# Adaptive-layernorm block: down products taken two or four token tiles at a time, their 64-row remainders on different rows, the last layernorm in two parts, stores from four buffers

## The chip, the cores and the metric

The kernel runs on one NeuronCore of one Trainium2 chip. The metric is the device time of one execution in microseconds. Lower is better.

## The reference

One transformer block with adaptive layernorm, for a batch of 2 sequences of 1024 tokens of 256 features, in float32 throughout. A vector `c` gives shift, scale and gate rows by one product; then come causal attention with 16 heads of 128 and a gated feed-forward part whose weights are integers with a scale for each output row. Cut to what matters:

```python
sa, ca, ga, sb, cb, gb = silu(c) @ wmod            # ga, gb kept at least 0.25 from zero
h = layernorm(x) * (1 + ca) + sa
x = x + ga * attention(h, Wq, bq, Wk, bk, Wv, bv, Wo, bo)   # rotary, causal softmax
h = layernorm(x) * (1 + cb) + sb
gate = silu(h @ ((wq_gate - 128) * s_gate[:, None]).T)      # 256 -> 704
up = h @ ((wq_up - 128) * s_up[:, None]).T                  # 256 -> 704
x = x + gb * ((gate * up) @ ((wq_down - 128) * s_down[:, None]).T)   # 704 -> 256
```

The hidden width is 704 = 5 x 128 + 64. That remainder of 64 is what much of the change is about.

## The kernel before, in words

The order of all work is written out by hand: every engine executes its instructions in the order in which the program text issues them, and a wait holds up all that stands behind it on the same engine. SP's queue issues the loads, the transposing copies of the attention and the stores; ACT's queue issues some loads.

*Attention.* The main loop (L644 to L684) goes over 32 units (batch, pair of heads, head) and in each over eight query tiles of 128 tokens. For each tile, TensorE makes scores, DVE masks them and finds the maximum, ACT takes the exponential, DVE turns 32x32 blocks, and SP's copies finish the transposition into `pT`. `values` multiplies it with v into the bank `po`, `project_out` adds the output product to the residual `x[b]` (L482, on DVE). Projections for the next unit, and pieces listed in `extras`, fill the loop.

*Feed-forward.* Tokens go in four blocks of 512: (batch 0, block 0), (0, 1), (1, 0), (1, 1). For each block `ln_turn` (L206) transposes the normalized tiles `xn` on TensorE into two banks of `ps_a`, and DVE applies the modulation (L217) into `h2`. `hidden(b, blk, c)` (L495) makes chunk c of the 704 hidden features for 512 tokens: gate and up products (L508), silu on ACT (L522), product of both on DVE (L523) into `gT`. The last chunk, c = 5, holds 64 gate rows and 64 up rows in one bank, and its product (L520) goes to rows 0 to 63 of `gT`. `down(b, blk, j)` (L525) multiplies the `gT` of one token tile of 128 with the scaled down weights `wdT` in six contractions, five over 128 rows and one over 64, into a bank `pd`; DVE adds the residual into `yo` (L538), and SP stores it (L539). `yo` comes from the two buffers "r1" of the pool `rot`.

The down weights reach the chip with their last 64 rows repeated (L775), and `ffn_down_scale` scales all 128 rows of every chunk, so rows 64 to 127 of `wdT`'s last chunk hold a copy of rows 0 to 63 already.

*Banks.* `bank` (L466) hands out four accumulation banks in turn: one of `ps_y`, one of `ps_o`, two of `ps_a`. The transposes of `ln_turn` take the same two of `ps_a`. The gate and up products of the tail have two double banks of `ps_sc`.

*The tail* (L686 to L718) starts when the last unit's scores are done, near 985 us. It interleaves `hidden(0, 1, c)` with the last output products, then does `values` of the last unit (TensorE from 1001.25 us on), chunk 4, four output products, chunk 5. Then DVE takes the statistics of all eight token tiles of batch 1 (`ln_stats`), ACT the root for all (`ln_sqrt`), and the four down tiles of block (0, 0) run with `ln_scale` and `ln_turn` of (1, 0) between. In the chunks of block (1, 0) stand `ln_turn` of (1, 1), after chunk 0, and one down tile of (0, 1) after each of the chunks 1 to 4; in the chunks of (1, 1) one down tile of (1, 0) each in the same places. The four down tiles of (1, 1) end the program:

```python
        for c in range(NF):
            hidden(1, 1, c)
            if c in (1, 2, 3, 4):
                down(1, 0, c - 1)
        for j in range(4):
            down(1, 1, j)
```

Block (0, 0) of the feed-forward part runs its `hidden` chunks inside the last attention unit (L677).

Of the kernel before, what the change touches and what calls it, by code (L numbers as in the profile page):

```python
# [11 lines left out]
F32 = mybir.dt.float32  # L12
I32 = mybir.dt.int32
AF = mybir.ActivationFunctionType
ALU = mybir.AluOpType
PSUM = bass.MemoryType.PSUM

P = 128
B, S, D = 2, 1024, 256
H, DH = 16, 128  # L20
HID = 704
NT = S // P
# [15 lines left out]
def adaln_block(ctx: ExitStack, tc: tile.TileContext, a, cos_d, sin_d, out):  # L38
# [427 lines left out]
    def bank(name):  # L466

        pool, tag = banks[turn[0] % 4]
        turn[0] += 1
        return pool.tile([P, 512], F32, tag=tag, name=name)  # L470

    def project_out(u, t, late=False):

        b, g, h = u
        if t % 4 == 0:
            nc.vector.reciprocal(rdens[u][:, t : t + 4], dens[u][:, t : t + 4])  # L476
        name = f"py_{b}{g}{h}{t}"
        py = bank(name) if late else ps_y.tile([P, 512], F32, tag="y", name=name)
        nc.tensor.matmul(  # L479
            py[:, :D], outs[u][:, ts(t, P)], weights[b, g]["o"][:, h, :], start=True, stop=True  # L480
        )
        nc.vector.scalar_tensor_tensor(  # L482
            x[b][:, t, :], py[:, :D], rdens[u][:, t : t + 1], x[b][:, t, :], ALU.mult, ALU.add
        )
# [10 lines left out]
    def hidden(b, blk, c, late=True):  # L495
        if c == 0:
            gTs[b, blk] = fpool.tile([P, NF, QB], F32, tag="f", name=f"gT_{b}{blk}")
        last = c == NF - 1
        if late:
            pg = ps_sc.tile([P, S], F32, tag="sc", name=f"pgu_{b}{blk}{c}")  # L500
            pgs = [pg[:, ts(j, QB)] for j in range(2)]
        else:
            pgs = [
                ps_a.tile([P, 512], F32, tag="a", name=f"pgu_{b}{blk}{c}{j}") for j in range(2 - last)
            ]
        for pg, n in zip(pgs, ("gate",) if last else ("gate", "up")):
            for k in range(KC):
                nc.tensor.matmul(  # L508
                    pg,
                    wT["last"][:, k, :] if last else wT[n][:, k, ts(c, P)],  # L510
                    h2s[b, blk][:, k, :],
                    start=(k == 0),
                    stop=(k == KC - 1),
                )
        sg = ppool.tile([P, QB], F32, tag="p", name=f"sg_{b}{blk}{c}")
        if last:

            m = HID - FULL
            nc.scalar.activation(sg[m:], pgs[0][:m], AF.Silu)
            nc.vector.tensor_tensor(gTs[b, blk][:m, c, :], sg[m:], pgs[0][m:], ALU.mult)  # L520
        else:
            nc.scalar.activation(sg, pgs[0], AF.Silu)  # L522
            nc.vector.tensor_tensor(gTs[b, blk][:, c, :], sg, pgs[1], ALU.mult)  # L523

    def down(b, blk, j):  # L525
        t = blk * 4 + j
        pd = bank(f"pd_{b}{t}")
        for c in range(NF):
            m = min(P, HID - c * P)
            nc.tensor.matmul(  # L530
                pd[:, :D],
                gTs[b, blk][:m, c, ts(j, P)],
                wdT[b][:m, c, :],
                start=(c == 0),
                stop=(c == NF - 1),
            )
        yo = rot.tile([P, D], F32, tag="r1", name=f"yo_{b}{t}")
        nc.vector.tensor_tensor(yo, pd[:, :D], x[b][:, t, :], ALU.add)  # L538
        nc.sync.dma_start(out[b, ts(t, P), :], yo)  # L539


    units = [(b, g, h) for b in range(B) for g in range(NG) for h in range(HG)]
# [52 lines left out]
    with tc.manual_schedule():  # L595
        nc.scalar.activation(
            sc.rearrange("p b k -> p (b k)"), sc.rearrange("p b k -> p (b k)"), AF.Silu
        )
        nc.scalar.activation(warm, eps_t, AF.Sqrt)
        weights[0, 0] = {}  # L600
        load_w(0, 0, "q")
        load_w(0, 0, "k")
        for t, t_d in ((cos_t, cos_d), (sin_t, sin_d)):
            nc.sync.dma_start(t[:, :QB], t_d[:, :QB])
        load_w(0, 0, "v")
        for t in (4, 6):
            load_x(0, t, 2, nc.sync)
        for t, t_d in ((cos_t, cos_d), (sin_t, sin_d)):
            nc.sync.dma_start(t[:, QB:], t_d[:, QB:])
        nc.sync.dma_start(wga, a["w_gates"])  # L610
        nc.sync.dma_start(wmod[:, 1], a["L0_wmod"][1])
        load_proj(*units[2][:2])
        load_out(0, 0)
        nc.gpsimd.memset(bvacc, 0.0)

        for blk, t in enumerate(t32):
            for j in range(3):
                nc.gpsimd.memset(t[:, :, j, 4 * blk + j + 1 :, :], 0.0)
        for t in (0, 2):
            for j in range(2):  # L620
                ln_stats(0, "a", t + j)
            ln_sqrt(0, "a", t, t + 2)
            if t:
                ln_scale(0, "a", 0, (0, 1))
        modulation(0, ps_y, "y")
        ln_scale(0, "a", 0, (2, 3))
        shift_scale(0)
        ln_turn(0, "a", 0, 0, new_hT(0, 0), split=True)
        for t in range(4, NT):
            ln_stats(0, "a", t)  # L630
        ln_sqrt(0, "a", 4, NT)
        for s in ("q", "k"):
            project_qk(units[0], s, 0)
        for t in (0, 2):
            project_v(0, 0, t, *((ps_o, "o"), (ps_y, "y"))[t // 2])
        ln_scale(0, "a", 1)
        release()
        ln_turn(0, "a", 1, 0, new_hT(0, 1), split=True)
        gates()
        for s in ("q", "k"):  # L640
            project_qk(units[0], s, 1)
        nc.gpsimd.dma_start(bo_bc, a["L0_attn_bo"].to_broadcast([P, D]))

        for n, u in enumerate(units):  # L644
            b, g, h = u
            prev = units[n - 1] if n else None
            nxt = units[n + 1] if n + 1 < N else None
            nb, ng = (b, g + 1) if g + 1 < NG else (b + 1, 0)
            more = nb < B
            for i in range(NT):  # L650
                ps, nmax = score(u, i)
                if i >= 1:
                    turned(u, i - 1)
                elif prev:
                    turned(prev, NT - 1)
                expo(u, i, ps, nmax)

                if i < 4 and n > 1:
                    project_out(units[n - 2], 4 + i)
                if i >= 4 and prev:  # L660
                    project_out(prev, i - 4)
                release()
                if i in (1, 3, 4, 6) and nxt:
                    project_qk(nxt, *{1: ("q", 0), 3: ("k", 0), 4: ("q", 1), 6: ("k", 1)}[i])
                if i in (5, 6) and prev:
                    values(prev, 1, 4 * (i - 5), 4 * (i - 4))

                if i == 7 and prev:
                    values(u, 0, 0, 4)
                if n == 1 and i == 1:  # L670
                    values(prev, 0, 0, 4)
                if i in (0, 2):
                    if h == 0:
                        project_v(b, g, 4 + i)
                    elif more:
                        project_v(nb, ng, i)
                if not nxt and 1 <= i < 7:  # L677
                    hidden(0, 0, i - 1, late=False)
                extras(n, i)
                if i == 7 and h == 1:  # L680
                    if more:
                        load_out(nb, ng)
                    if n + 3 < N:
                        load_proj(*units[n + 3][:2])  # L684

        u, prev = units[-1], units[-2]  # L686
        turned(u, 7)
        for c in range(4):
            hidden(0, 1, c)
            project_out(prev, 4 + c, late=True)  # L690
            project_out(u, c, late=True)
        values(u, 1, 0, 8)
        hidden(0, 1, 4)
        for t in range(4, NT):
            project_out(u, t, late=True)
        hidden(0, 1, 5)
        for t in range(NT):
            ln_stats(1, "b", t)
        ln_sqrt(1, "b", 0, NT)
        down(0, 0, 0)  # L700
        ln_scale(1, "b", 0)
        down(0, 0, 1)
        down(0, 0, 2)
        ln_turn(1, "b", 0, 2, new_h2(1, 0))
        down(0, 0, 3)
        ln_scale(1, "b", 1)
        for c in range(NF):
            hidden(1, 0, c)
            if c == 0:
                ln_turn(1, "b", 1, 2, new_h2(1, 1))  # L710
            if c in (1, 2, 3, 4):
                down(0, 1, c - 1)
        for c in range(NF):
            hidden(1, 1, c)
            if c in (1, 2, 3, 4):
                down(1, 0, c - 1)
        for j in range(4):
            down(1, 1, j)  # L718


def _rotary_tables():
# [65 lines left out]
```

## Time and profile before

| | |
|---|---|
| time, median of 3 runs | 1104.93 us (1104.89 to 1105.02) |
| profiled execution | 1106.62 us, its span 1104.9 us |
| granted TensorE clock in it | 0.998 of full speed |
| silu products on ACT after 1000 us, 512 columns | 0.597 us each |
| layernorm statistics on DVE after 1000 us (bn_stats, then bn_aggr) | 0.399 and 0.182 us each |
| table load of ACT before root and silu | 1.283 us each |
| `yo` on DVE (128x256) | 0.424 us each |
| product of the last chunk on DVE (64x512) | 0.690 us each |
| store of one `yo`, issue to landing | 1.7 us (median) |

The span goes from the first to the last instruction. A float32 matmul of the program stands in the trace as two records, each with its own weight load (PEld). The ends of matmul records are modelled and overlap, so the distance of starts tells more than the busy time. Every row of the timeline gives start, duration, engine, line, operation and, in brackets, the idle time of the engine before it and what ended that. In forms such as `64*128` the first number is the rows of the array in use, the second its columns.

### The profile page before, as it was taken

The page shows a single profiled execution, that of the slowest core. Times are in us where ns is not written, and L with a number is a line of the kernel's source. Part 1 is how long each engine was busy: PE and PEld are TensorE (multiplying, and loading weights), DVE is VectorE, ACT ScalarE, POOL GpSimd, SP SyncE. Part 2 cuts the span into 40 slices and gives each one's busy share as a digit, 9 for nine tenths or more (in the row PEclk, how much of TensorE's full clock was granted, in tenths as well). Part 3 has the DMA queues.
Part 4 walks back from the last instruction along what each step waited for, and adds up shares of the span by engine and source line. Part 5 has one row for each costly group of instructions (what it writes and reads, how often), then busy time and mean ns, then how long its engine had stood idle before and what let it go on. Part 6 is the DMA issues. An engine that isn't in the chain of part 4 may idle for free.

```text
span 1104.9 us, 12352 instructions
## 1 busy us (share of the span) xinstructions
PE 1092.1 (99%) x3556; PEld 645.3 (58%) x3556; DVE 643.0 (58%) x1406; ACT 508.5 (46%) x953; POOL 391.8 (35%) x356
## 2 busy tenths in 40 slices
PE   9999999999999999999999999999999999999998
PEld 5555555555666565555555656656565555455555
DVE  5556565666566666865566566555656757544311
ACT  5644444554555445354454455444444454641110
POOL 4635353535353433444333543333433433000000
PEclk9999999999999999999999999999999999999999
DMA  6365656556556655265654546454545455331000
GB/s 213 83 146 126 162 117 167 144 119 146 127 144 143 146 112 134 65 145 115 142 125 110 143 110 145 108 143 109 139 101 139 97 118 115 85 79 32 24 19 29
DMA packets 65656, 128.88 MB, mean 117 GB/s; under 512 B 18451, under 2 KB 22803, under 8 KB 65589
## 3 DMA queue, kind: packets, MB, share of 16 engines
q1 hardware_dynamic: 63236, 123.81, 47.5%
q10 hardware_dynamic: 2304, 4.16, 1.1%
q8 instruction: 29, 0.48, 0.2%
q14 instruction: 39, 0.31, 0.1%
q0 software_dynamic: 48, 0.13, 0.1%
HBM read 25.26 MB, written 2.10 MB: 25 GB/s over the span
## 4 chain that ended last, share of the span: by engine, by line
PE 97%; DVE 3%; issue 0%; ACT 0%; POOL 0%; DVEq 0%; ACTq 0%; POOLq 0%
PE ps L392 22%; PE po L453 22%; PE py L479 10%; PE pq L349 10%; PE pk L349 10%; PE pv L331 9%; PE pgu L508 7%; PE pd L530 4%; DVE t L426 1%; PE warm_ps L82 1%; DVE ps L395 1%; PE pm L119 0%; PE ptx_a L210 0%; DVE x L482 0%; DVE kT L365 0%
## 5 line engine op out<-in xcount | busy, mean ns | idle before, releaser
L395 DVE CUSTOM_DVE_ANT_0 ps<-ps,mask 128x128 f32<-128x128 f32 (+7 forms) x256 | 195.7, 764 | 328.9 <-PE ps L392 328.5
L412 ACT ACTIVATE p<-ps,nmax 128x128 f32<-128x128 f32 (+7 forms) x256 | 189.7, 741 | 345.8 <-DVE nmax L395 342.4
L392 PE MATMUL ps<-kT,qT 128*128 128x512 f32 (+3 forms) x768 | 289.7, 486 | 0.7 <-ACT p L412 0.7
L453 PE MATMUL po<-pT,v 128*128 128x512 f32 (+3 forms) x768 | 263.3, 486 | 0.0
L392 PEld LDWEIGHTS ps<-kT,qT 128*128 128x128 f32 x768 | 140.9, 190 | 127.2 <-issue 120.8
L453 PEld LDWEIGHTS po<-pT,v 128*128 128x128 f32 x768 | 145.9, 190 | 115.4 <-issue 91.8
L426 DVE STREAM_TRANSPOSE t<-p 128x128 f32<-128x128 f32 (+7 forms) x256 | 198.2, 774 | 1.0 <-ACT p L412 0.7
L479 PE MATMUL py<-wo,o 128*128 128x256 f32 x512 | 157.2, 391 | 1.5 <-DVE x L482 1.5
L362 POOL TENSOR_TENSOR r_k<-r_k,sin_t 128x512 f32<-128x512 f32 x64 | 81.3, 1271 | 209.8 <-ACT r_k L361 209.7
L368 POOL TENSOR_TENSOR kT<-kT,r_k 128x512 f32<-128x512 f32 x64 | 81.5, 1273 | 162.7 <-DVE kT L365 148.3
L362 POOL TENSOR_TENSOR r_q<-r_q,sin_t 128x512 f32<-128x512 f32 x64 | 81.8, 1277 | 150.8 <-ACT r_q L361 147.1
L479 PEld LDWEIGHTS py<-wo,o 128*128 128x128 f32 x512 | 90.0, 190 | 61.2 <-issue 30.9
L331 PE MATMUL pv<-wv,hT 128*128 128x256 f32 x512 | 120.9, 379 | 1.1 <-DVE qT L365 1.1
L349 PE MATMUL pq<-hT,wq 128*128 128x512 f32 x256 | 120.6, 593 | 0.5 <-DVE hT L217 0.5
L482 DVE SCALAR_TENSOR_TENSOR x<-py,rden,x 128x256 f32<-128x256 f32 x256 | 115.9, 455 | 8.0 <-DVE rden L476 0.9
L349 PE MATMUL pk<-hT,wk 128*128 128x512 f32 x256 | 120.3, 592 | 0.0
L361 ACT ACTIVATE r_q<-pq,cols 64x512 f32<-64x512 f32 x128 | 87.4, 683 | 48.1 <-PE pq L349 47.2
L331 PEld LDWEIGHTS pv<-wv,hT 128*128 128x128 f32 x512 | 97.1, 190 | 15.2 <-DVE qT L365 1.2
L361 ACT ACTIVATE r_k<-pk,cols 64x512 f32<-64x512 f32 x128 | 87.4, 683 | 18.0 <-PE pk L349 15.9
L368 POOL TENSOR_TENSOR qT<-qT,r_q 128x512 f32<-128x512 f32 x64 | 83.7, 1308 | 25.3 <-DVE qT L365 20.7
L349 PEld LDWEIGHTS pk<-hT,wk 128*128 128x128 f32 x256 | 48.6, 190 | 35.8 <-issue 32.0
L349 PEld LDWEIGHTS pq<-hT,wq 128*128 128x128 f32 x256 | 48.3, 190 | 35.7 <-issue 31.2
(83 smaller groups left out, 704.6 us busy)
## 6 DMA issues: line engine op xcount, KB each, us to landing
pT<-t SPq DMA_DIRECT2D x512, 128.0 KB, 2.4
pT<-t SPq DMA_DIRECT2D x512, 64.0 KB, 2.0
wq<-in_Wq SPq DMA_DIRECT2D x16, 256.0 KB, 3.0
wk<-in_Wk SPq DMA_DIRECT2D x16, 256.0 KB, 4.1
wv<-in_Wv SPq DMA_DIRECT2D x16, 256.0 KB, 4.3
wo<-in_Wo SPq DMA_DIRECT2D x16, 256.0 KB, 2.9
out<-yo SPq DMA_DIRECT2D x16, 128.0 KB, 1.7
x<-in_x SPq DMA_DIRECT2D x4, 256.0 KB, 5.1
```

The costliest lines, as they stand in the source:

```text
L331: nc.tensor.matmul(pv[:, ts(j, HG * DH)], hT[b, n][:, k, ts(r, P)], weights[b, g]["v"][:, k, :], start=(k == 0), stop=(k == KC - 1),)
L349: nc.tensor.matmul(pq, weights[b, g][s][:, k, ts(h, DH)], hT[b, n][:, k, :], start=(k == 0), stop=(k == KC - 1),)
L361: nc.scalar.activation(r1[to], pq[of], AF.Identity, bias=cols[of, c : c + 1])
L362: nc.gpsimd.tensor_tensor(r1, r1, sin_t[:, sl], ALU.mult)
L368: nc.gpsimd.tensor_tensor(dst[:, sl], dst[:, sl], r1, ALU.add)
L392: nc.tensor.matmul(ps[:, c:e], qT[:, ts(i, P)], kT[:, c:e], start=True, stop=True)
L395: nc.vector.tensor_tensor_reduce(ps[:, :L], ps[:, :L], mask[:, NT - 1 - i :, :].rearrange("p t k -> p (t k)"), -SCALE, FLT_MAX, ALU.add, A ...
L412: nc.scalar.activation(p[:, :L], ps[:, :L], AF.Exp, bias=nmax, scale=-1.0, accum_out=dens[u][:, i : i + 1])
L426: nc.vector.transpose(t32[blk][:, :, j, : i + 1, :].rearrange("p c k b -> p k c b"), p[:, : (i + 1) * P].rearrange("p (k c a) -> p k c a", ...
L453: nc.tensor.matmul(po[:, off * P :], vs[b, g][:, k, ts(h, DH)], pT[:, off:, :, k, :], start=(k == 0), stop=(k == last),)
L479: nc.tensor.matmul(py[:, :D], outs[u][:, ts(t, P)], weights[b, g]["o"][:, h, :], start=True, stop=True)
L482: nc.vector.scalar_tensor_tensor(x[b][:, t, :], py[:, :D], rdens[u][:, t : t + 1], x[b][:, t, :], ALU.mult, ALU.add)
```

## The change

- `hidden` (last chunk): the product goes to both halves of the rows of `gT`. The token tiles of even number within the block go to rows 0 to 63, those of odd number to rows 64 to 127. Two instructions of 64x256 take the place of one of 64x512.
- `down` takes several token tiles. First it issues the five 128-row contractions of every tile, each into its own bank, then the 64-row contractions of all tiles, on rows 0 to 63 for even tiles and 64 to 127 for odd ones, then the additions and stores.
- `yo` comes from the four buffers "xn" of the pool `xnp`, except for block (0, 0).
- The layernorm of batch 1 is made in two parts: statistics, root and scaling of its first four token tiles stand before and after `values`, their `ln_turn` after chunk 5 of (0, 1); the other four follow.
- Down tiles are called in pairs for (0, 0) and (1, 1), by four after chunk 3 for (0, 1) and (1, 0). `ln_turn` of (1, 1) comes before the chunks of (1, 0).

The diff, with line numbers of the kernel after left out:

```diff
@@ hidden
-            nc.vector.tensor_tensor(gTs[b, blk][:m, c, :], sg[m:], pgs[0][m:], ALU.mult)
+            for j, rows_ in enumerate((slice(0, m), slice(m, P))):
+                part = lambda t: t.rearrange("p (t j q) -> p t j q", j=2, q=P)[:, :, j, :]
+                nc.vector.tensor_tensor(
+                    part(gTs[b, blk][rows_, c, :]), part(sg[m:]), part(pgs[0][m:]), ALU.mult
+                )
@@ down
-    def down(b, blk, j):
-        t = blk * 4 + j
-        pd = bank(f"pd_{b}{t}")
-        for c in range(NF):
-            m = min(P, HID - c * P)
+    def down(b, blk, *js):
+        pds = {}
+        for j in js:
+            pds[j] = bank(f"pd_{b}{blk}{j}")
+            for c in range(NF - 1):
+                nc.tensor.matmul(
+                    pds[j][:, :D],
+                    gTs[b, blk][:, c, ts(j, P)],
+                    wdT[b][:, c, :],
+                    start=(c == 0),
+                    stop=False,
+                )
+        for j in js:
+            half = ts(j % 2, HID - FULL)
             nc.tensor.matmul(
-                pd[:, :D],
-                gTs[b, blk][:m, c, ts(j, P)],
-                wdT[b][:m, c, :],
-                start=(c == 0),
-                stop=(c == NF - 1),
+                pds[j][:, :D],
+                gTs[b, blk][half, NF - 1, ts(j, P)],
+                wdT[b][half, NF - 1, :],
+                start=False,
+                stop=True,
             )
-        yo = rot.tile([P, D], F32, tag="r1", name=f"yo_{b}{t}")
-        nc.vector.tensor_tensor(yo, pd[:, :D], x[b][:, t, :], ALU.add)
-        nc.sync.dma_start(out[b, ts(t, P), :], yo)
+        for j in js:
+            t = blk * 4 + j
+            if (b, blk) == (0, 0):
+                yo = rot.tile([P, D], F32, tag="r1", name=f"yo_{b}{t}")
+            else:
+                yo = xnp.tile([P, D], F32, tag="xn", name=f"yo_{b}{t}")
+            nc.vector.tensor_tensor(yo, pds[j][:, :D], x[b][:, t, :], ALU.add)
+            nc.sync.dma_start(out[b, ts(t, P), :], yo)
@@ tail
+        for t in range(4):
+            ln_stats(1, "b", t)
+        ln_sqrt(1, "b", 0, 4)
         values(u, 1, 0, 8)
+        ln_scale(1, "b", 0)
         hidden(0, 1, 4)
         for t in range(4, NT):
             project_out(u, t, late=True)
         hidden(0, 1, 5)
-        for t in range(NT):
+        ln_turn(1, "b", 0, 2, new_h2(1, 0))
+        for t in range(4, NT):
             ln_stats(1, "b", t)
-        ln_sqrt(1, "b", 0, NT)
-        down(0, 0, 0)
-        ln_scale(1, "b", 0)
-        down(0, 0, 1)
-        down(0, 0, 2)
-        ln_turn(1, "b", 0, 2, new_h2(1, 0))
-        down(0, 0, 3)
+        ln_sqrt(1, "b", 4, NT)
+        down(0, 0, 0, 1)
         ln_scale(1, "b", 1)
+        down(0, 0, 2, 3)
+        ln_turn(1, "b", 1, 2, new_h2(1, 1))
         for c in range(NF):
             hidden(1, 0, c)
-            if c == 0:
-                ln_turn(1, "b", 1, 2, new_h2(1, 1))
-            if c in (1, 2, 3, 4):
-                down(0, 1, c - 1)
+            if c == 3:
+                down(0, 1, 0, 1, 2, 3)
         for c in range(NF):
             hidden(1, 1, c)
-            if c in (1, 2, 3, 4):
-                down(1, 0, c - 1)
-        for j in range(4):
-            down(1, 1, j)
+            if c == 3:
+                down(1, 0, 0, 1, 2, 3)
+        down(1, 1, 0, 1)
+        down(1, 1, 2, 3)
```

## Prediction

> **What bounds the kernel now.** I read the page's busy shares and the chain that ended last first:
>
> ```profile
> PE 1092.1 (99%) x3556; PEld 645.3 (58%) x3556; DVE 643.0 (58%) x1406; ACT 508.5 (46%) x953; POOL 391.8 (35%) x356
> PE 97%; DVE 3%; issue 0%; ACT 0%; POOL 0%; DVEq 0%; ACTq 0%; POOLq 0%
> ```
>
> TensorE is never without work, and it is 97% of the chain; DVE, ACT, POOL and SP matter only where TensorE waits for them. So an edit is worth what it does to the spacing of matmuls. The diff touches what follows 1001 us (and one DVE product before it). The chain in order of time, from 1000 us on, has in this stretch:
>
> ```profile
> 1010.44 1.73 PE py L479 x8
> 1012.17 1.72 PE pgu L508 x4
> 1013.88 8.75 PE pd L530 x36
> 1022.63 0.60 PE ptx_b L210 x4
> 1023.23 0.03 issue
> 1023.26 0.82 DVE h L217
> 1024.08 0.04 issue
> 1024.12 3.05 PE pd L530 x12
> ```
>
> DVE is on the chain once (L217), 0.82 us; all else is matmuls. How closely those follow each other I read from the weight loads in the timeline (start, duration), since the ends of matmuls are modelled and their busy times overlap:
>
> ```profile
> 1050.66 0.30 PEld L508 LDWEIGHTS pgu<-h,wgateT 128*128 128x128 f32 x2 [0.33 <-issue]
> 1051.20 0.19 PEld L508 LDWEIGHTS pgu<-h,wgateT 128*128 128x128 f32 x1 [0.24 <-issue]
> 1051.62 0.19 PEld L508 LDWEIGHTS pgu<-h,wgateT 128*128 128x128 f32 x1 [0.24 <-issue]
> ...
> 1054.20 1.92 PEld L530 LDWEIGHTS pd<-wdT,gT 128*128 128x128 f32 x9 [0.24 <-issue]
> 1056.45 0.29 PEld L530 LDWEIGHTS pd<-wdT,gT 64*128 64x128 f32 x2 [0.33 <-issue]
> 1057.07 0.30 PEld L508 LDWEIGHTS pgu<-h,wlastT 128*128 128x128 f32 x2 [0.33 <-issue]
> ```
>
> Each matmul of the program is two records, each with a load. A 512-column record comes every 0.43 us (1051.62 less 1051.20, 0.429 by the unrounded starts), a 256-column one every 0.216 ((1.92-0.19)/8). From 1050.66 to 1057.07 lie one up/gate chunk (8 records) and one down tile (12): 6.41 us, of which 8 x 0.429 + 12 x 0.216 = 6.02 are matmuls. The other 0.39 us is the passage to 64 rows and back: at both edges the loads stand apart (0.33 instead of 0.24 idle, then two loads 0.11 apart), so the array ran empty and a load lay bare. In the last stage the 64-row loads start at 1091.96, 1094.94, 1097.92: 2.98 a tile, again 12 x 0.216 + 0.39.
>
> **1. Fewer passages.** The 16 down tiles pay 16 x 0.39. After, six calls of down (pair, pair, four, four, pair, pair) pay 6: 10 x 0.39 = **3.9 us** off, all on TensorE's path.
>
> **2. 64-row contractions next to each other, on rows 0-63 and 64-127.** No row of before shows two such matmuls in flight together, so bounds. If nothing overlaps, 0 (a 64-row record costs its 0.216, as in the 2.98 above). If each even/odd couple runs wholly together, 8 couples x 2 records x 0.216 = 3.45. The Trainium skill (TensorE: Matmul & The Clock Gate, Part 3) says that matmuls on different row groups run concurrently, some 4 ns apart, but also that matmuls start and end in strict program order. The second sentence speaks against a full halving here: the order is a1 a2 b1 b2, b1 can only join a2, and a pair takes 3 slots instead of 4, a call of four 5 instead of 8. Four pairs save 4 x 0.216, two fours 2 x 3 x 0.216: **2.15 us**. By the row alone (each 64-row matmul behind the last) it would be 0. I take the rule's 2.15, because the 64-row weight loads follow each other in 0.11 us, twice as fast as the matmuls, so loads need not stop it. The same skill (TensorEngine Tiling, Key Properties) says that changing the mode, not the tile, drains the array; so I charge going from one half to the other nothing, and keep the 0.39 at the edges of a call. Whether a change of half costs something is the rival below.
>
> **3. Last layernorm, first half moved up.** Four statistics (0.53 us each in before's row of eight: 2.1), one sqrt (0.3), reciprocal 0.17 and four scalings 1.38 now stand before and beside `values(u, 1)`, 5.6 us of TensorE. DVE has the room; in before it waits 8.41 us there:
>
> ```profile
> 1010.48 0.60 ACT L522 ACTIVATE sg<-pgu 128x512 f32<-128x512 f32 x1 [2.85 <-PE pgu L508]
> 1011.11 0.69 DVE L523 TENSOR_TENSOR gT<-sg,pgu 128x512 f32<-128x512 f32 x1 [8.41 <-ACT sg L522]
> 1011.71 0.17 DVE L476 RECIPROCAL rden<-den 128x4 f32<-128x4 f32 x1
> ...
> 1011.99 1.66 DVE L482 SCALAR_TENSOR_TENSOR x<-py,rden,x 128x256 f32<-128x256 f32 x4
> ```
>
> Price 0 with this cover; 4 us of DVE without it. But the sqrt throws out ACT's silu table, and the order of the built program has the reload holding the wait for TensorE, so it can't run early. The same pattern stands in before:
>
> ```profile
> 987.74 1.28 ACT L522 ACT_TABLE_LOAD   x1 [2.10 <-PE pgu L508]
> ...
> 989.04 0.60 ACT L522 ACTIVATE sg<-pgu 128x512 f32<-128x512 f32 x1
> ```
>
> So the silu of chunk 4 comes not at 1010.48 but 1.33 later (load 1.28, its start 0.05). Queued behind it on DVE: product gT (to 1012.5+0.7), then the four L482 (13.33 to 14.99). New is who waits: the transposes of `ln_turn`, which now follow hidden chunk 5 and take the two ps_a banks that the third and fourth L482 empty. TensorE is ready at 1013.72; the third L482 ends at 14.60, the transposes start at 14.66: a **new wait of 0.94**. The fourth L482 ends (14.99) while the first four transposes run. The other three table loads hide (sqrt's carry no wait; the one of hidden(1,0,0) is there before too, and its product ends some 0.6 us before chunk 2 wants the bank).
>
> The down pair begins near 1015.5. DVE meanwhile does two gT products, two h (0.77 each) and four statistics, to 1019.5; the pair's first 64-row matmul ends past 1020. Nothing waits. The second pair's two ps_a banks are then emptied by yo 2 and 3, and the second `ln_turn` wants them at once: yo 2 can start 0.04 after the first contraction is done, takes 0.42, and TensorE, ready at 26.12, starts at 26.5: **new wait of 0.37**. The old stall goes: from 1013.72 to 1027.11 and on to the next bare load, 13.49 us hold 48 x 0.216 + 8 transposes at 0.109 + 4 x 0.39 = 12.8, so about **0.7** was waiting (the bank behind yo, then L217 in the chain above). Net of part 3: -0.94 - 0.37 + 0.7 = **-0.6 us**. Bounds: -1.2 (nothing of the old stall was removable) to +0.7 (the new waits vanish).
>
> **4. The split product.** The last chunk's 64x512 product (690 ns) becomes two of 64x256. Nearest row: 424 ns for yo, 128x256 out of PSUM; at worst 690 each. I take 0.42, so 0.15 us more, four times. In the attention stage the next score's DVE work starts 0.15 later, but `values(u, 1)` needs its result only some 10 us later; in the tail 20 records (4.3 us) of down now stand between the product and its reader, where before it was 10. Cost 0, at most 0.15 each if bare.
>
> **5. Stores.** With four tiles a call, four yo need four buffers; xn's are free by then (their transposes are over before the first call of four, and a store lands 1.7 us after its issue, against 6 us and more between calls). SP has nothing else in its queue after the pT copies: 0.33 each, 0. At the very end, though, two yo follow the last contractions where one did. In slots, a2 ends 0.216 before b2, yo is 0.42, so the last yo ends **0.2 us** later. The store after it is the same.
>
> **Sum.** 3.9 + 2.15 - 0.6 - 0.2 = 5.25; following the record starts stage by stage (start of tail 0.66, two fours 1.83 each, end 1.23 - 0.2) gives 5.35. Take 5.3. The profiled execution has a span of 1104.9 (1106.62 with what lies around it); the median of runs is 1104.93, equal to the span, so I subtract there: **1099.6 us**, 0.48% less.
>
> **Rivals.**
> *No overlap in the array.* Then part 2 is 0; the last yo and the second ln_turn wait come back a bit (0.2 and 0.2): 3.5 off, 1101.4. For it: no row of before shows overlap, and f32 needs two loads for each matmul. Against: the rule of part 2.
> *Full overlap of each couple* (b1 beside a1): 1.3 more, some of it lost to the yo waits: about 6.5 off, 1098.4. Against: program order.
> *Slower: going from one half of the rows to the other drains the array like a change of mode.* Within the calls there are 4 x 1 + 2 x 3 = 10 such changes. At 0.2 each (half of the 0.39 round trip) no overlap is left and 3.5 - 2.0 = 1.5 remain: 1103.4, no change that can be told. It decides from 3.5/10 = 0.35 us each; at 0.6 (drain, bare load and a wait for the first half's results to be written) it is 2.5 slower: 1107.4. For it: the trace shows that these small passages cost as much as two records. Against: before's cost is there only at a change of 64 to 128.
> *It does not do what it says,* that is the waits of part 3 grow: the silu's reload could hold more; each 1 us there is 1 us of the sum, and it would take 5 to cancel it.
>
> **How the numbers follow.** Forecast 0.50 (1099.6); no overlap 0.25 (1101.4); full overlap 0.12 (1098.4); half changes at about 0.2: 0.06 (1103.4); slower by them 0.04; waits of part 3 much larger 0.03. The range 1098.0 to 1101.8 holds the first three with 0.2 to 0.4 of spread. A measurement of this kernel can tell about 0.2% (2.2 us) from no change: faster 0.87, same 0.08, slower 0.05.
>
> **What would show it.** Passages: 64-row weight loads in six clusters instead of 16, with 128-row loads at 0.216 between. Overlap: in a call of four, eight 64-row matmuls whose starts span about 0.9 us (1.5 without overlap), b1 with a2. Part 3: an ACT table load of 1.28 near 1010.5 with a wait on pgu, transposes started by L482 near 1014.6, and again by yo near 1026.5. End: two yo 0.4 apart, and the last load of weights near 1095.5. It is wrong if the 64-row matmuls stand 0.3 or more apart at each change of half, or if TensorE waits over 2 us before the first transposes.

## The result, and the profile after

| | before | changed |
|---|---|---|
| median of 6 runs each | 1104.97 us (1104.74 to 1105.17) | 1099.3 us (1098.75 to 1100.49) |
| ratio of the times | | 0.9951, 95% interval 0.9939 to 0.9962 |
| profiled execution, span | 1106.62, 1104.9 us | 1100.49, 1098.7 us |
| first matmul of the last `values` to the last matmul | 99.97 us | 93.47 us |
| last matmul's start to the end of the span | 3.63 us | 4.11 us |

The kernel is 5.7 us faster by the medians, 6.1 by the two profiled spans. Some executions, these two profiled ones among them, contain a stretch of 3.4 us in which the granted clock is half; it lies ahead of the part that the change touches and moves the whole time by some 1.4 us. Therefore the last two rows of the table are what I compare below; they are worked out from the starts of records in the traces: 6.50 us less and 0.48 more, 6.02 us gained. I call the first of them the tail and the second the end. A slot is the 0.216 us at which 256-column records follow each other.

The changed kernel's chain in order of time, as far as it answers to the one of before (start, duration, what):

```profile
1010.38 0.03 issue
1010.41 1.28 ACT L527
1011.70 0.61 ACT sg L527
1012.33 0.69 DVE gT L528
...
1013.21 1.28 DVE x L482 x3
1014.49 0.04 issue
1014.54 1.09 PE ptx_b L210 x8
1015.63 4.32 PE pd L536 x20
1019.95 0.63 PE pd L545 x4
1020.58 4.51 PE pd L536 x20
1025.10 0.68 PE pd L545 x4
1025.78 0.42 DVE yo L558
1026.19 0.04 issue
1026.24 1.09 PE ptx_b L210 x8
1027.33 13.73 PE pgu L508 x32
1041.07 8.63 PE pd L536 x40
1049.70 1.06 PE pd L545 x8
```

The long rows of L536 and L545 show the grouping: eight 64-row records take 1.06 us of the chain. New on it is a detour over ACT and DVE from 1010.41 to 1014.5: ACT's load of the silu table, silu, its product and three residual additions, and only then the transposes. In before the chain had only matmuls there. At 1025.78 it runs over `yo` before the second set of transposes.

The 64-row part of a call of four, on TensorE in the timeline, with the record ahead of it and behind it:

```profile
1049.32 0.38 PE L536 MATMUL pd<-wdT,gT 128*128 128x256 f32 x1
1049.63 1.13 PE L545 MATMUL pd<-wdT,gT 64*128 64x256 f32 x8
1050.69 0.70 PE L508 MATMUL pgu<-h,wgateT 128*128 128x512 f32 x1
```

From 1049.63 to 1050.69 pass 1.06 us for eight records. The passage to 64 rows and back has a part in that: of its 0.39, 0.09 stand before the first of them (0.31 from the start of the record ahead, instead of a slot) and 0.10 after 1050.69, which leaves 0.20. The remaining 0.86 are four slots. By their unrounded starts the eight stand in four couples, 6 to 7 ns apart within each (1049.630 and 1049.636, 1049.950 and 1049.956, 1050.166 and 1050.172, 1050.381 and 1050.388): the two halves of the array work side by side, as same_rows below confirms.

### The profile page after: what moved, and what is told of

Same layout as the page of the kernel before. It is cut to its first block, busy times and chain, and to the rows that moved or that the text cites. A ratio compares the mean times of both kernels' runs of the same rounds, so it can differ in the third digit from the quotient of the medians.

```text
span 1098.7 us, 12359 instructions
## 1 busy us (share of the span) xinstructions
PE 1084.5 (99%) x3556; PEld 643.9 (59%) x3556; DVE 643.1 (59%) x1410; ACT 511.4 (47%) x956; POOL 391.9 (36%) x356
## 4 chain that ended last, share of the span: by engine, by line
PE 96%; DVE 3%; ACT 0%; issue 0%; DVEq 0%; POOL 0%; ACTq 0%; POOLq 0%
PE ps L392 22%; PE po L453 22%; PE py L479 10%; PE pq L349 10%; PE pk L349 10%; PE pv L331 9%; PE pgu L508 7%; PE pd L536 3%; DVE t L426 1%; PE warm_ps L82 1%; DVE ps L395 1%; PE pd L545 0%; DVE x L482 0%; PE ptx_b L210 0%; PE pm L119 0%; PE ptx_a L210 0%
```

## Experiments

In the expectations, "changed kernel" is the one of the diff above. They speak of spans; since the half-clock stretch is in some profiled executions and not in others, each is judged by the tail and the end. All times with an interval are ratios to the kernel before, on the same chip.

| run | tail | end | both, against the changed kernel's 97.58 | median | ratio, 95% interval |
|---|---|---|---|---|---|
| same_rows | 96.46 | 3.67 | +2.55 | 1101.73 | 0.9962 (0.9949 to 0.9975) |
| halves_apart | 93.48 | 4.10 | 0.0 | 1099.2 | 0.9935 (0.992 to 0.9949) |
| one_by_one | 100.37 | 3.62 | +6.41 | 1105.58 | 1.0 (0.9992 to 1.0009) |
| ln_late | 93.28 | 4.11 | -0.19 | 1099.08 | 0.9933 (0.9916 to 0.9949) |
| early_table | 92.48 | 4.10 | -1.00 | 1098.83 | 0.9934 (0.9919 to 0.9949) |
| turn_later | 92.10 | 4.11 | -1.37 | 1099.26 | 0.9934 (0.9917 to 0.995) |
| two_buffers | 93.47 | 4.10 | 0.0 | 1099.01 | 0.9937 (0.9922 to 0.9952) |
| four_calls | 91.56 | 4.00 | -2.02 | 1097.16 | 0.9921 (0.9906 to 0.9935) |
| zero_rows | 94.04 | 3.63 | +0.09 | 1100.21 | 0.9949 (0.9934 to 0.9964) |
| last_full | 91.78 | 3.63 | -2.17 | 1098.02 | 0.9925 (0.9909 to 0.9942) |

My theory: what costs in before is the passage to 64 rows and back (0.39 a tile), the second gain is that the halves of the array overlap, and the layernorm's earlier start brings new waits of its own. Rivals: the overlap is worth nothing, the passage is not what costs, or the earlier layernorm is what gains.

**Overlap taken away (same_rows).**

```diff
-            half = ts(j % 2, HID - FULL)
+            half = slice(0, HID - FULL)
```

and the product of the last chunk is one instruction of DVE again, into rows 0 to 63 (that part of the edit is left out here).

> The changed kernel, but every 64-row contraction stands on rows 0 to 63 (and the last chunk's product is one DVE instruction again); calls by pairs and fours stay. If the overlap of the two halves is worth what the starts in the trace of the changed kernel show (8 couples x 2 records x 0.216 = 3.45 us), the time rises by that, less what comes back where yo no longer ends for two tiles at once (about 0.4 at the second ln_turn, 0.35 at the end): about 2.7 more, span near 1101.4. If the overlap is only apparent and the gain is from fewer passages to 64 rows alone, the span stays at 1098.7.

Measured +2.55: the tail 2.99 longer, the end 0.44 shorter. The 64-row part of a call of four now takes twice the slots:

```profile
1048.68 1.99 PE L541 MATMUL pd<-wdT,gT 64*128 64x256 f32 x8
1050.60 0.70 PE L508 MATMUL pgu<-h,wgateT 128*128 128x512 f32 x1
```

1.92 us to the next product instead of 1.06: 0.86 more, four slots of 0.216. The overlap is real; the rival of no overlap falls.

**Two contractions of one half ahead of two of the other (halves_apart).**

```diff
-        for j in js:
+        for j in sorted(js, key=lambda j: (j % 2, j)):
             half = ts(j % 2, HID - FULL)
```

> The changed kernel, but in the two calls of four the 64-row contractions come in the order of tiles 0, 2, 1, 3, so two on rows 0 to 63 and then two on rows 64 to 127. If the two halves of the array take work independently of program order, still 4 slots of 0.216: no change, span 1098.7. If order is kept and a whole matmul with both its records is the unit, the third contraction can only join the second: 6 slots instead of 4, two calls x 2 x 0.216 = 0.9 more, 1099.6. If order is kept by the single record, 7 slots: 1.3 more, 1100.0.

```profile
1048.16 1.14 PE L545 MATMUL pd<-wdT,gT 64*128 64x256 f32 x8
1049.23 0.70 PE L508 MATMUL pgu<-h,wgateT 128*128 128x512 f32 x1
```

1.07 us from the first to the next product, and the tail is 93.48: still four slots. Two contractions of the same half don't overlap (same_rows has eight slots for eight records), so to be done in four slots the third in the program, the first of the other half, must have started with the first, ahead of the second. Across halves the starts do not keep the order of the program; within a half it can't be told apart. The records stand in couples 13 to 14 ns apart here, against 6 to 7.

The signals of completion do keep that order, by the trace's events of TensorE's semaphore. In this call three records raise it: those that start at 1048.477 and 1048.491, which end the first couple of contractions, and one of the last couple. The first raise comes at 1048.867, 0.39 us after its record's start, as in the changed kernel. The second comes only at 1049.316, 0.83 us after its record's start, when the other couple is done too (last starts at 1048.909 and 1048.922). So the contraction that started ahead of its turn is told of in its turn. This also speaks against another reading, that the built program had the four in alternating order after all: then the second raise would follow the first by some 0.04 us, as it does in the changed kernel (1050.340 and 1050.382). DVE's four `yo` show the wait; the changed kernel first, then this one:

```profile
1050.36 1.42 DVE L558 TENSOR_TENSOR yo<-pd,x 128x256 f32<-128x256 f32 x4 [7.94 <-PE pd L545]
1048.89 1.54 DVE L558 TENSOR_TENSOR yo<-pd,x 128x256 f32<-128x256 f32 x4 [7.94 <-PE pd L545]
```

**One tile for each call (one_by_one).** The four-tile and two-tile calls become single ones in the same places, for instance

```diff
-                down(0, 1, 0, 1, 2, 3)
+                for j in range(4):
+                    down(0, 1, j)
```

> The changed kernel, with alternating halves and the early layernorm, but each down tile is a call of its own (in the same places). By the account of 0.39 for each passage and full overlap of couples: 10 x 0.39 + 3.45 = 7.35 more, less about 0.35 at the end and 0.5 at the second ln_turn: 6.5 more, span near 1105.2. If alternating halves alone gives the overlap (the next tile's loads running under the last contraction), or passages are cheap when only the tile changes, less than 3 more.

Measured +6.41. Halves that alternate but do not stand next to each other bring nothing: each tile still goes out of and into 128 rows on its own. The chain has 2.98 us for a tile, as in before:

```profile
1017.00 2.35 PE pd L536 x10
1019.35 0.63 PE pd L545 x2
1019.98 2.36 PE pd L536 x10
```

This kernel has 16 passages like the kernel before, no overlap, but the new layernorm, and its tail is 0.40 longer than before's 99.97. By the starts of records the two tails differ only around the transposes of the layernorm: 0.98 us are lost at the first ones and 0.15 at the second, and before's stall of 0.74 is gone. So the layernorm in two parts is by itself a loss, in this order of calls 0.4 us.

**The layernorm in one part again (ln_late).** After chunk 5 of (0, 1), with the lines that go left out:

```diff
+        for t in range(NT):
+            ln_stats(1, "b", t)
+        ln_sqrt(1, "b", 0, NT)
         down(0, 0, 0, 1)
+        ln_scale(1, "b", 0)
         down(0, 0, 2, 3)
+        ln_turn(1, "b", 0, 2, new_h2(1, 0))
+        ln_scale(1, "b", 1)
```

with the second `ln_turn` after chunk 0 of (1, 0), as in before.

> The changed kernel with its grouped down calls, but the last layernorm is begun in one part after hidden chunk 5, as in the kernel before. By my account the early part brings a wait of 0.93 (silu's table load) at the first transposes; without it that goes, while the wait for yo at the first ln_turn (0.6) stays and one for h before the next gate products of about 0.5 comes: 0.4 less, span near 1098.3. If beginning early is itself worth something, it is slower than the changed kernel, by up to the 0.7 that waited in the kernel before: 1099.4.

Measured -0.19; I had expected -0.4. Its chain shows which waits took the place of ACT's:

```profile
1024.62 0.68 PE pd L545 x4
1025.76 0.67 PE ptx_b L210 x4
1026.45 0.82 DVE h L217
1027.41 3.67 PE pgu L508 x8
```

The transposes wait for `yo` (between 1025.30 and 1025.76), and the gate products for `h`. By the traces it is slightly faster with the late layernorm (halves_apart and two_buffers repeat the changed kernel's tail to within 0.02 us; the medians are too coarse for a difference of 0.2). So the rival, that beginning early gains, falls for this order of calls.

**The silu table loaded early (early_table).**

```diff
         ln_sqrt(1, "b", 0, 4)
+        nc.scalar.activation(warm, ones[:, :1], AF.Silu)
         values(u, 1, 0, 8)
```

> The changed kernel with one dummy silu of one column on ACT right after the first root, so that the silu table is loaded while TensorE is in values and not after hidden chunk 4. If that load is what makes the first transposes wait, their wait of 0.93 goes: span near 1097.8. If DVE's own queue (statistics and scalings moved up) is what makes them late, nothing changes: 1098.7.

Measured -1.00. In its timeline the load stands at another place:

```profile
1003.91 1.28 ACT L716 ACT_TABLE_LOAD   x1
...
1009.28 0.60 ACT L527 ACTIVATE sg<-pgu 128x512 f32<-128x512 f32 x1 [2.91 <-PE pgu L508]
1009.91 0.69 DVE L528 TENSOR_TENSOR gT<-sg,pgu 128x512 f32<-128x512 f32 x1 [4.38 <-ACT sg L527]
```

In the changed kernel the same load sits between the end of the products and silu, because it carries the wait:

```profile
1010.41 1.28 ACT L527 ACT_TABLE_LOAD   x1 [2.89 <-PE pgu L508]
1011.70 0.60 ACT L527 ACTIVATE sg<-pgu 128x512 f32<-128x512 f32 x1
...
1014.54 1.09 PE L210 MATMUL ptx_b<-ident,xn_b 128*128 128x128 f32 x8 [0.77 <-DVE x L482]
```

The same 1.28 us of ACT is free in one place and makes TensorE wait in the other. The wait was caused by the load, not by DVE's queue: with the load away, silu follows its products at once and the transposes stand where TensorE is ready for them.

**The first transposes after the first down pair (turn_later).**

```diff
-        ln_turn(1, "b", 0, 2, new_h2(1, 0))
         ...
         down(0, 0, 0, 1)
+        ln_turn(1, "b", 0, 2, new_h2(1, 0))
         ln_scale(1, "b", 1)
+        turn[0] += 2
         down(0, 0, 2, 3)
```

> The changed kernel, but ln_turn of the first half stands after the first down pair, and the second pair takes the banks of ps_y and ps_o, not those of ps_a. Nothing is waited for at hidden chunk 5 but the first of the four residual additions (about 0.1), and both ps_a banks are long free at the second ln_turn: of the waits of 0.93 and 0.58, 1.3 to 1.4 go, span near 1097.3. If the wait for silu only moves to the down products, or DVE cannot turn the banks over in time, under 0.5 is gained.

The line with `turn` hands the next down products the other two banks. Measured -1.37, of the 0.93 and 0.58 that waited. Here ACT's load is as late as in the changed kernel, 9.27 us after the first matmul of the last `values` in both; what TensorE does next, the down products, doesn't need the two banks that are late.

**Two buffers for the stores (two_buffers).**

```diff
-            if (b, blk) == (0, 0):
-                yo = rot.tile([P, D], F32, tag="r1", name=f"yo_{b}{t}")
-            else:
-                yo = xnp.tile([P, D], F32, tag="xn", name=f"yo_{b}{t}")
+            yo = rot.tile([P, D], F32, tag="r1", name=f"yo_{b}{t}")
```

> The changed kernel with every yo from the two buffers of rot instead of four of xnp for the calls after the first. By my account stores are hidden: the third and fourth yo of a call of four wait some 2 us for a store, but DVE's next product is wanted only 4 us later: no change, 1098.7. If the wait on DVE reaches TensorE through gT and the pgu banks, 0.5 to 1 more for each call of four: 1099.7 to 1100.7.

No change in tail or end. DVE does wait for the stores, in the timeline after a call of four:

```profile
1048.84 0.76 DVE L555 TENSOR_TENSOR yo<-pd,x 128x256 f32<-128x256 f32 x2 [7.94 <-PE pd L545]
1051.12 0.91 DVE L555 TENSOR_TENSOR yo<-pd,x 128x256 f32<-128x256 f32 x2 [1.53 <-DMA out<-yo]
1053.54 0.69 DVE L528 TENSOR_TENSOR gT<-sg,pgu 128x512 f32<-128x512 f32 x1 [1.51 <-ACT sg L527]
```

1.53 us for a store, but then it is idle for another 1.51 us before its next product. So four buffers are worth nothing here.

**The waits taken away together (four_calls).** The dummy silu after both roots, `ln_scale` of the second half ahead of the down products, all four tiles of (0, 0) in one call, the second `ln_turn` after chunk 1 of (1, 0), and the very last store issued from ACT's queue (the first dummy silu and the store are left out here):

```diff
+        nc.scalar.activation(warm, ones[:, :1], AF.Silu)
         ln_scale(1, "b", 1)
-        down(0, 0, 0, 1)
-        down(0, 0, 2, 3)
-        ln_turn(1, "b", 1, 2, new_h2(1, 1))
+        down(0, 0, 0, 1, 2, 3)
         for c in range(NF):
             hidden(1, 0, c)
+            if c == 1:
+                ln_turn(1, "b", 1, 2, new_h2(1, 1))
```

> A version that takes the waits away: the dummy silu after both roots, all four down tiles of the first block in one call, the second ln_turn after the chunk 1 of the next block, the very last store issued from ACT's queue. Expected against the changed kernel: 0.93 and 0.58 of waits and one passage of 0.39, and about 0.1 at the last store: 2.0 less, span near 1096.7. If ACT's and DVE's waits reappear elsewhere (the two r1 buffers hold DVE for a store), about 1 less.

Measured -2.02, as expected (0.11 of it at the end). The chain between chunk 5 and the next block has no engine but TensorE:

```profile
1010.64 1.72 PE pgu L508 x4
1012.36 0.87 PE ptx_b L210 x8
1013.24 8.63 PE pd L536 x40
1021.87 1.06 PE pd L545 x8
1022.93 7.06 PE pgu L508 x16
```

**Zeros instead of 64 rows (zero_rows).** The kernel before, with

```diff
+            nc.gpsimd.memset(gTs[b, blk][HID - FULL :, NF - 1, :], 0.0)
@@ down
-            m = min(P, HID - c * P)
             nc.tensor.matmul(
                 pd[:, :D],
-                gTs[b, blk][:m, c, ts(j, P)],
-                wdT[b][:m, c, :],
+                gTs[b, blk][:, c, ts(j, P)],
+                wdT[b][:, c, :],
```

> The kernel before, with one change: rows 64 to 127 of the last chunk's gT are set to zero (by GpSimd, when the block's gT is begun) and the last contraction of each down tile goes over all 128 rows. Nothing is grouped or overlapped. If it is the passage to 64 rows and back that costs 0.39 a tile, all 16 go: about 6.1 less from the first matmul of the last values to the last matmul of the program, 93.9 instead of 99.97 us, as much as the whole change brings, with the end as in the kernel before. If a sixth contraction costs that by itself (semaphores, a last load), nothing changes: 99.97.

Tail 94.04, that is 5.93 less than before. The chain has down tiles of 12 records at 12 x 0.216:

```profile
1033.87 2.59 PE pd L530 x12
1036.46 3.43 PE pgu L509 x8
1039.89 2.59 PE pd L530 x12
1042.48 3.43 PE pgu L509 x8
```

A tile and a chunk take 6.02 us where they took 6.41. So the cost in before was the passage, 0.39 each, and not the sixth contraction; and multiplying by 64 rows of zeros, with the order of calls and the layernorm of before, gains as much as the whole change (tail and end 97.67 against 97.58).

**The last two tiles over 128 rows (last_full).** As four_calls, but the last two tiles of the program are single, with zeros in the other half of their `gT` columns, and the last store is on SP.

> The version of four calls, but the last two down tiles of the program are separate and contract all 128 rows with zeros in the other half, and the last store is on SP again. The last matmul comes 0.2 later (two records more, one passage less), but only one yo and one store follow it: 3.63 instead of 4.00 us from the last matmul to the end. Together 0.15 to 0.2 less than the version of four calls. If the end is set by the stores' landing and not by yo, it is 0.2 slower.

The last matmul comes 0.22 later and the end is 0.37 shorter: 95.41 against 95.56, 0.15 less, as expected. Medians and intervals of the two don't tell them apart. By the traces its tail and end together are the shortest that ran; by the medians four_calls stands first. Against the changed kernel the trace gives four_calls 2.02 us, and the executions without the half-clock stretch agree: 1096.88 to 1097.17 us against 1098.75 to 1099.32. The ratios of the two can't be set against each other, since the executions of before that they stand on differ in the half-clock stretch.

## Why the prediction was right

The time forecast, 1099.6, and the measured 1099.3 agree, and the gain comes from the two causes that were named, fewer passages and overlap. The sizes of the second and of the waits were off, in opposite directions. The terms, each against what the runs show:

1. *Fewer passages, 3.9 us.* Right: before's tile carried 0.39 (zero_rows takes exactly that away: 6.41 to 6.02), and the changed kernel has six clusters of 64-row records. What is asserted of the drain by the Trainium skill (TensorEngine Tiling, Key Properties), that it comes with a change of mode and not of tile, agrees: inside the calls, going between halves costs nothing that could be seen.
2. *Overlap, 2.15 us.* That halves overlap was right, and the size was off: it is 3.45 by the starts (8 couples x 2 records x 0.216), 2.99 in the tail with what the waits for `yo` take back, by same_rows. The term that failed is "the order is a1 a2 b1 b2, b1 can only join a2". I let a sentence of the skill (TensorE: Matmul & The Clock Gate, Part 3: matmuls start and end in strict program order) set the number of slots. halves_apart shows that the starts don't keep that order across halves, and the measurement decides; of the ends its semaphore events agree with the sentence. The rival of full overlap, which I gave 0.12, describes the array rightly.
3. *Layernorm, -0.6 us.* The first wait is there, for the reason given: the last product record starts at 1013.179, the transposes at 1014.536, 0.93 more than a record's 0.429; I had 0.94. The second is 0.58 (0.888 from the last contraction to the transposes, less 0.306 in the passages without a wait), where I had 0.37: with full overlap both tiles end at once, so `yo` starts no earlier than the end of the call. Net -0.8 by my account of 0.7 for the old wait; one_by_one gives -0.4 without pairs, and ln_late -0.2 against its own later waits. All have the same sign: this part of the change costs.
4. *Split product, 0.* Right: 422 to 425 ns each, and TensorE waited for none of them.
5. *Stores, 0, and 0.2 us at the end.* Four buffers are worth 0 (two_buffers). The end grew by 0.48, not 0.2: both last tiles are done at once, the second `yo` starts 0.34 after the first, and SP issues the second store behind the first:

```profile
1094.28 0.70 PE L545 MATMUL pd<-wdT,gT 64*128 64x256 f32 x4
1095.02 0.76 DVE L558 TENSOR_TENSOR yo<-pd,x 128x256 f32<-128x256 f32 x2 [4.39 <-PE pd L545]
1095.47 0.81 SPq L559 DMA_DIRECT2D out<-yo  x2
```

In before one `yo` and one issue of 0.33 followed. It is the same fault as in 2, I had spaced the tiles by a slot; and I had left out that the second store waits for the issue of the first.

With the measured terms: 3.9 + 3.45 - 0.93 - 0.58 + 0.7 - 0.48 = 6.06, against 6.02 by the table. So an overlap taken too small (1.3) was partly balanced by waits taken too small (0.5), and what was left (6.02 against 5.3) was halved by the medians, which show 0.35 us less gain than the traces. That forecast and median agree to 0.3 us is therefore in part luck.

That the span of the profiled execution equalled the median was chance: 1.7 us lie outside the span, and the profiled execution had the half-clock stretch of some 1.4 us, which the timed ones of the table, by their times, did not have. Nothing hung on it, since it was the median from which the gain had to be taken.

The slower rival, a drain at each change of half, falls with the 6 to 7 ns between the two of a couple.

## What to carry to other kernels

Look at the starts of weight loads around a contraction that is shorter than the array: where they stand apart on both sides, the passage costs time (0.39 us here), while the short contraction took as many slots as a full one. Filling up with zeros takes all passages away; grouping such contractions, on different rows, takes most of them and adds the overlap. Grouping ends several tiles at once, so whoever empties their banks must not be needed by the next matmuls or by the end. And when work is moved to an engine's idle time, ask what state it leaves behind: a root between two silus cost ACT only idle time but TensorE 0.93 us, until the reload was put where nobody waited for ACT.

## What the runs showed of the hardware that was not expected

*Row halves start out of program order and are told of in order,* as shown above: with two contractions of one half ahead of two of the other, all four still took four slots, and the one that had started ahead of its turn raised its semaphore 0.83 us after its last record's start instead of 0.43. So what was said ahead of every engine, that it executes in the order of the program text, does not hold on TensorE for the starts of matmuls on different halves of the rows.

*A stretch at half the clock in some executions.* In the profile of before, in stretches from 942.0, from 945.7 and from 949.1 us (busy time of each engine with the number of instructions, then the granted clock, the share of the DMA engines and GB/s):

```profile
942.00:945.60 3.60, 1.63 (x9) 1.05 (x10) 3.50 (x8) 0.46 (x2) 0.95 (x1) 1.00 0.00 0
945.70:949.10 3.40, 3.40 (x6) 1.45 (x6) 2.10 (x6) 0.56 (x2) 0.00 (x0) 0.50 0.87 193
949.10:953.00 3.90, 3.90 (x12) 2.02 (x11) 1.37 (x4) 1.95 (x3) 0.00 (x0) 1.00 0.93 202
```

TensorE had 1.63 us of work in the 3.6 us before, waiting for DVE (1.30 us for `xn_b`, 0.81 for `x`); then it had the half clock for 3.4 us, and six matmul records where same_rows has nine in the same stretch. But same_rows had hardly more work before it (1.68 us), and kept the full clock:

```profile
942.00:945.60 3.60, 1.68 (x9) 1.10 (x10) 3.50 (x8) 0.46 (x2) 0.90 (x1) 1.00 0.00 0
945.70:949.10 3.40, 3.38 (x9) 1.47 (x9) 2.05 (x6) 1.45 (x3) 0.00 (x0) 1.00 0.87 193
```

Of the twelve profiled executions, before, changed, turn_later and zero_rows had it there; the last `values` begin at 1001.1 to 1001.4 in those, at 999.6 to 1000.0 in the six with neither. The other two, ln_late and last_full, had 6.8 us of it from about 8.6 us on instead, and begin at 1002.5 and 1002.8. The program up to there is the same in all but small things, and the kernel before, in 16 executions on one chip, had a mean granted clock of 0.998 in eight (1106.1 to 1107.4 us) and of 1.0 in the other eight (1104.9 to 1105.5). So which executions have the stretch varies with one and the same kernel, and the gap near 943 us alone does not bring it. What decides it, and whether filling the gap would end it, was not tried.
